# Normalising attention probabilities in place on GpSimd, instead of scaling the outputs by turned reciprocals

## The chip, the cores and the metric

The kernel runs on one core of one Trainium2 chip. The metric is the device time of one execution in microseconds: the median of several runs. All arrays are float32.

## What is computed

A normalised input goes through an attention layer and through a gated feed-forward branch (called FFN here); the output is the input plus the product of the two. The part that the change touches is the attention, with 4 sequences of 1024 tokens, 16 query heads of width 64 over 4 key heads, a causal window of 512 keys and 4 sink keys:

```python
att = jnp.einsum('bkgqd,bkjd->bkgqj', q, k) * scale
mask = _sliding_window_sink_mask(t)   # causal & j >= i - 511, or j < 4
att = jnp.where(mask[None, None, None, :, :], att, -jnp.inf)
att = jax.nn.softmax(att, axis=-1)
y = jnp.einsum('bkgqj,bkjd->bkgqd', att, v)
y = y.reshape(b, N_HEAD, t, HS).transpose(0, 2, 1, 3).reshape(b, t, c)
return y @ Wo.T
```

The softmax divides each row of exponentials by its sum. Since that division is by row (by query), it can be done on the exponentials before the second product, or on the product after it.

## The kernel before

The program has three stages: projections (up to about 949 us), attention with the recurrent FFN streamed beside it (949 to about 1745 us), and the output product with the gate. The change lies in the second stage, and in the few lines at the end of the first that prepare its first step.

**Steps.** A tile is 128 queries of one sequence. Tiles are taken in pairs (`PAIRED`): a far tile (5th to 8th of its sequence), which sees 512 window keys and 4 sink keys, 516 columns (`OWN`), and a near tile (1st to 4th), which sees 1 to 4 key tiles, 128 to 512 columns. The pair of sequence `b` and number `t` holds far tile 7 - t and near tile t, so the near tile has t + 1 key tiles. Each pair is worked off in four steps: two values of `m` (which pair of key heads) by two of `rp` (which pair of query heads in a group). So there are 16 pairs, 64 steps (`order`), numbered here from 0. Each step has, for each of its two tiles, four heads `(r, g)`: `r` is the query head of the pair, `g` the key head. "The first pair" is r = 0, both g.

**What a step does for a tile.** `scored` multiplies queries by keys into the PSUM tile `S` on TensorE (L299). For a far tile `merged` copies the own key tile's scores over the oldest one where the mask wants it (VectorE, L314). `maxed` adds the mask, scales, takes the row maximum and writes the result to the SBUF tile `pr` (VectorE, L335). `powered` takes the exponentials in place and their row sums into `sums` (ScalarE, L346, with a second instruction that reads the accumulator). `turned` transposes blocks of 128 keys of `pr` on TensorE into the PSUM tile `T`, two half transposes for each block and head (L365, `t<-ident,pr`), and copies them to SBUF as `pT` (ScalarE, L383). `values` multiplies `pT` by the values into a PSUM bank `yp` that the two tiles of the step share (L411). The far tile needs two things more: `led` makes a masked copy `lead` of its first key block (VectorE, L397), and `values_apart` adds the sink keys' share (L427) and `lead`'s share (L411).

**Normalising.** The exponentials are not divided. `inverted` takes the reciprocals of all 8 sums of the step in one instruction (VectorE, L475) and spreads each over 64 columns in SBUF (GpSimd, L477, 512 columns). `turned_extras` transposes five blocks of 128 columns in ten half transposes (L365): `held`, which holds the far tile's exponentials of the sink keys (copied out by `sinks_kept`, GpSimd, L354), and the four spread blocks. Its inner function `kept` copies the result to SBUF as the tile `extras`, named `e` in the profile (ScalarE, L497). `values_apart` reads the first block; `stored` multiplies `yp` by the other blocks on its way to SBUF (VectorE, L440). `sent` sends a finished tile's `y` to DRAM (GpSimd's queue, L447) after the second of two steps.

**Order.** The order on TensorE, VectorE, ScalarE and GpSimd is written out by hand (`tc.manual_schedule`), each engine works its list strictly in order, and the step's loop interleaves the values of step p with the scores and exponentials of step p + 1 (`far_next`, `near_next`). `streamed` puts blocks of the FFN between them (weights by DMA, products L1099); `small_products` and a few VectorE and GpSimd instructions (among them the small `trs` of L115) belong to it too.

There are two forms of a step. When the next near tile has one or two key tiles (`ride`), its scores ride in the free columns of the next far tile's `S`, and all four of its exponentials are taken before the step ends. The extras' transposes then go to the PSUM tile `T` (named `et` in the profile), and `kept` follows at once. This is called a riding step here. Otherwise, and in the last step, the form is a plain step: the near tile's scores have an `S` of their own at the step's end, the fourth of its exponentials is taken at the start of the following step, and the extras' transposes go into the free columns of the next far tile's `S`, where `kept` follows after `merged` and before `maxed`. `S`, `T` and `yp` are single tiles that each use must find released.

Of the kernel before, what the change touches and what calls it, by code (L numbers as in the profile page):

```python
# [8 lines left out]
F32 = mybir.dt.float32  # L9
AF = mybir.ActivationFunctionType  # L10
ALU = mybir.AluOpType
# [4 lines left out]
P = 128  # L16
N_HEAD = 16
N_KV = 4
HS = 64
WINDOW = 512  # L20
# [24 lines left out]
def recurrent_block_kernel(  # L45
# [206 lines left out]
    class Step:  # L252


        def __init__(self, i, m, rp, sums):
# [17 lines left out]
            self.sums = sums  # L273
            self.maxima = {}
            self.pT = {}

# [65 lines left out]
        def powered(self, *heads):  # L342

            for r, g in heads:
                low = self.pr[:, g, r, : self.cols]
                nc.scalar.activation(  # L346
                    low, low, AF.Exp, bias=self.maxima.pop((r, g)), scale=-1.0,
                    accum_out=self.sums[:, r, g : g + 1],
                )

        def sinks_kept(self):
# [71 lines left out]
        def values_apart(self):  # L423

            for r in range(PAIR):
                for _, rows, cols in self.quads():
                    nc.tensor.matmul(  # L427
                        self.y[rows, r * P : (r + 1) * P],
                        sink_values[self.b][:, r, cols], self.extras[:, 0, :],
                        start=False, stop=False, skip_group_check=True,  # L430
                    )
# [12 lines left out]

        def sent(self):
            if (self.rp + 1) * PAIR == GROUP:
# [13 lines left out]
    def steps_of(tiles, m, rp):  # L460
        sums = pools["first"].tile(
            [P, 2, PAIR, 2], F32, tag="sums", name=f"s{tiles[0]}_{m}_{rp}", bufs=3
        )
        return [Step(i, m, rp, sums[:, at]) for at, i in enumerate(tiles)], sums

    def summed_in_one_bank(far, near):

        y = pools["ps_y"].tile([P, 2, PAIR * P], F32, tag="y", name=f"yp{far.name}")
        far.y, near.y = y[:, 0, :], y[:, 1, :]

    def inverted(steps, sums):

        name = steps[0].name
        inverse = pools["px"].tile([P, 2 * PAIR * 2], F32, tag="inverse", name=f"i{name}", bufs=2)
        nc.vector.reciprocal(inverse, sums.rearrange("p s r g -> p (s r g)"))  # L475
        spread = pools["px"].tile([P, 2 * PAIR * 2, HS], F32, tag="spread", name=f"r{name}", bufs=1)
        nc.gpsimd.tensor_copy(  # L477
            spread, inverse.unsqueeze(2).to_broadcast([P, 2 * PAIR * 2, HS])
        )
        return spread.rearrange("p (s g) c -> p s (g c)", g=2)  # L480

    def turned_extras(steps, spread, behind):

        far, near = steps
        parts = [far.held, *(spread[:, s, :] for s in range(2 * PAIR))]
        if behind is None:
            ps = pools["ps_t"].tile([P, 2, WIDE], F32, tag="T", name=f"et{far.name}")
        else:
            ps = behind.S[:, 0, :, SCOLS:]
        for slot, src in enumerate(parts):  # L490
            far.in_halves(ps, slot, src, P)
        extras = pools["px"].tile([P, len(parts), P], F32, tag="extras", name=f"e{far.name}", bufs=1)
        far.extras = extras
        far.scales, near.scales = extras[:, 1 : 1 + PAIR, :], extras[:, 1 + PAIR :, :]

        def kept():
            nc.scalar.copy(  # L497
                extras.rearrange("p s (h q) -> p h s q", h=2),
                ps[:, :, : len(parts) * HS].rearrange("p h (s q) -> p h s q", q=HS),
            )  # L500

        return kept
# [17 lines left out]
    with ExitStack() as a:  # L520
# [445 lines left out]
        with tc.manual_schedule():  # L966
# [4 lines left out]
            for at, (kind, pair) in enumerate(passes):  # L971
# [35 lines left out]
                for k, i in enumerate(OUTER):  # L1007
# [16 lines left out]
                    if end and k == 3:  # L1024
# [10 lines left out]
                        def scores(step, rs):  # L1035
# [5 lines left out]
                        first_scores = iter((  # L1041
                            lambda: scores(far, (0,)), lambda: scores(far, (1,)),
                            far.sinks_kept, lambda: scores(near, both),
                        ))
            for part in first_scores:
                part()
# [11 lines left out]
    with ExitStack() as a:  # L1058

        px = pools["px"] = a.enter_context(tc.tile_pool(name="px", bufs=1))  # L1060
        pools["odd"] = a.enter_context(tc.tile_pool(name="odd", bufs=1))
        ps_t = pools["ps_t"] = a.enter_context(tc.tile_pool(name="ps_t", bufs=1, space=PSUM))
        ps_f = a.enter_context(tc.tile_pool(name="ps_f", bufs=1, space=PSUM))
        pools["ps_y"] = a.enter_context(tc.tile_pool(name="ps_y", bufs=1, space=PSUM))
# [669 lines left out]
```

## Time and profile before

| | |
|---|---|
| median of 3 runs | 2138.59 us (2137.0 to 2141.21) |
| profiled execution | 2139.05 us |
| its span | 2137.3 us |
| mean granted TensorE clock | 0.995 |
| TensorE matmul busy | 2076.3 us (97%) |
| VectorE busy | 1495.8 us (70%) |
| ScalarE busy | 916.5 us (43%) |
| GpSimd busy | 448.4 us (21%) |

The page gives busy time, the chain of work that ended last, groups of instructions by line, and, for an idle engine, what ended the idle time. `PE` is TensorE's matmuls, `PEld` its weight loads, which overlap them, `DVE` VectorE, `ACT` ScalarE, `POOL` GpSimd, `SP` SyncE. In a group's row, `out<-in` are the program's names, then come shapes and count, then busy time and the mean of one in ns, then the idle time before the group and what ended it. In a timeline, a row has its start, its length, the engine and line, and in brackets the idle time of the engine before it with its releaser. Matmuls are pipelined and their ends are modelled, so a busy TensorE may still wait a little. Between 950 and 1700 us TensorE is busy nearly all of the time and GpSimd for 5 to 11 us in each 50.

### The profile page before, as it was taken

The page shows a single profiled execution, that of the slowest core. Times are in us where ns is not written, and L with a number is a line of the kernel's source. Part 1 is how long each engine was busy: PE and PEld are TensorE (multiplying, and loading weights), DVE is VectorE, ACT ScalarE, POOL GpSimd, SP SyncE. Part 2 cuts the span into 40 slices and gives each one's busy share as a digit, 9 for nine tenths or more (in the row PEclk, how much of TensorE's full clock was granted, in tenths as well). Part 3 has the DMA queues.
Part 4 walks back from the last instruction along what each step waited for, and adds up shares of the span by engine and source line. Part 5 has one row for each costly group of instructions (what it writes and reads, how often), then busy time and mean ns, then how long its engine had stood idle before and what let it go on. Part 6 is the DMA issues. An engine that isn't in the chain of part 4 may idle for free.

```text
span 2137.3 us, 43582 instructions
## 1 busy us (share of the span) xinstructions
PE 2076.3 (97%) x17586; PEld 1418.0 (66%) x17586; DVE 1495.8 (70%) x3092; ACT 916.5 (43%) x1840; POOL 448.4 (21%) x641
## 2 busy tenths in 40 slices
PE   7999999999999999999999999999999989999999
PEld 6888888888888888875555655555565544444443
DVE  5867588888877888876556555666665547777766
ACT  4343212111110000037777777777777744333332
POOL 3232315435241021141111111111111101111111
PEclk9999999999999999999999999999999999999999
DMA  8696322433554234258778988768578536666653
GB/s 297 248 370 218 104 99 99 163 114 124 224 188 138 99 110 166 79 190 290 261 237 240 319 250 243 256 198 301 185 251 284 182 146 180 167 169 191 172 157 98
DMA packets 215201, 417.20 MB, mean 195 GB/s; under 512 B 13796, under 2 KB 97844, under 8 KB 209880
## 3 DMA queue, kind: packets, MB, share of 16 engines
q1 hardware_dynamic: 171432, 266.12, 38.8%
q0 software_dynamic: 28288, 91.41, 13.8%
q10 hardware_dynamic: 15280, 56.89, 7.1%
q8 instruction: 138, 2.26, 0.4%
q14 instruction: 63, 0.52, 0.1%
HBM read 309.22 MB, written 121.93 MB: 202 GB/s over the span
## 4 chain that ended last, share of the span: by engine, by line
PE 83%; DVE 6%; issue 4%; ACT 4%; POOL 2%; DMA 1%; SPq 0%; ACTq 0%; POOLq 0%; DVEq 0%
PE u L1572 17%; PE u_q L899 16%; PE u_g L899 13%; PE S L299 10%; PE yp L411 8%; PE d_ps L1099 6%; PE t L365 5%; PE u L679 4%; PE yp L427 1%; DVE pr L335 1%; ACT pr L346 1%; ACT pT L383 1%; DVE t_g L915 1%; DVE f L852 1%; PE xtp L595 1%
## 5 line engine op out<-in xcount | busy, mean ns | idle before, releaser
L346 ACT ACTIVATE pr<-pr,nm 128x516 f32<-128x516 f32 (+4 forms) x512 | 325.5, 638 | 86.8 <-DVE nm L335 85.7
L335 DVE CUSTOM_DVE_ANT_0 pr<-S,near_mask 128x516 f32<-128x516 f32 (+4 forms) x512 | 275.7, 590 | 98.2 <-PE S L299 56.0
L383 ACT COPY pT<-t 128x1024 f32<-128x1024 f32 (+1 forms) x224 | 212.0, 946 | 116.5 <-PE t L365 114.5
L299 PE MATMUL S<-kT,qT 64*128 64x512 f32 (+4 forms) x1536 | 246.4, 446 | 4.0 <-DVE i L475 2.4
L411 PE MATMUL yp<-pT,v 128*32 128x256 f32 x3328 | 215.2, 382 | 5.1 <-ACT pT L383 4.5
L899 PE MATMUL u_q<-f,wq_again 128*128 128x256 f32 x896 | 203.2, 379 | 0.0
L899 PE MATMUL u_g<-wg,f 128*128 128x256 f32 x864 | 195.7, 380 | 4.5 <-DVE t_g L915 4.5
L365 PEld LDWEIGHTS t<-ident,pr 64*128 64x128 f32 x3328 | 126.1, 140 | 90.6 <-issue 68.6
L411 PEld LDWEIGHTS yp<-pT,v 128*32 128x32 f32 x3328 | 104.1, 110 | 123.4 <-issue 51.7
L899 PEld LDWEIGHTS u_q<-f,wq_again 128*128 128x128 f32 x896 | 170.0, 190 | 23.3
L899 PEld LDWEIGHTS u_g<-wg,f 128*128 128x128 f32 x864 | 163.8, 190 | 28.2 <-DVE t_g L915 6.2
L299 PEld LDWEIGHTS S<-kT,qT 64*128 64x128 f32 x1536 | 127.6, 190 | 79.2 <-issue 69.8
L1572 PE MATMUL u<-wo_sb,y 128*128 128x512 f32 x384 | 170.1, 592 | 0.5 <-DVE y L440 0.5
L365 PE MATMUL t<-ident,pr 64*128 64x64 f32 x3328 | 153.1, 230 | 4.0 <-ACT pr L346 1.8
L314 DVE COPY_PREDICATED S<-own_keys,S 128x256 f32<-128x256 uint32 x128 | 54.9, 429 | 131.2 <-PE S L299 92.3
L945 ACT COPY t_q<-u_q 128x512 f32<-128x512 f32 x28 | 16.4, 586 | 275.4 <-PE u_q L899 275.4
L1572 PEld LDWEIGHTS u<-wo_sb,y 128*128 128x128 f32 x384 | 72.9, 190 | 92.4 <-issue 91.4
L915 DVE TENSOR_TENSOR t_q<-u_q,t_q 128x512 f32<-128x512 f32 x128 | 88.2, 689 | 63.8 <-PE u_q L899 49.3
L915 DVE TENSOR_TENSOR t_g<-u_g,t_g 128x512 f32<-128x512 f32 x128 | 87.9, 687 | 40.8 <-PE u_g L899 35.8
L1572 PE MATMUL u<-wo_t,s 128*128 128x512 f32 x256 | 112.5, 592 | 0.0
L346 ACT ACTIVATION_READ_ACCUMULATOR pr<-pr,nm 128x1 f32 x512 | 96.6, 189 | 0.0
L477 POOL COPY r<-i 128x512 f32<-128x512 f32 x64 | 47.7, 745 | 217.4 <-DVE i L475 208.0
(284 smaller groups left out, 3560.6 us busy)
## 6 DMA issues: line engine op xcount, KB each, us to landing
d_w<-in_d_w_dram SPq DMA_DIRECT2D x128, 1024.0 KB, 8.0
xT<-xT_dram SPq DMA_DIRECT2D x24, 1024.0 KB, 5.6
xn<-in_x_dram ACTq DMA_DIRECT2D x34, 512.0 KB, 5.4
xT_dram<-xT POOLq DMA_DIRECT2D x32, 512.0 KB, 6.0
qT<-q_dram SPq DMA_DIRECT2D x64, 256.0 KB, 5.8
y_dram<-y POOLq DMA_DIRECT2D x64, 256.0 KB, 5.8
y<-y_dram SPq DMA_DIRECT2D x32, 512.0 KB, 5.3
g<-g_dram SPq DMA_DIRECT2D x32, 512.0 KB, 11.2
```

The costliest lines, as they stand in the source:

```text
L299: nc.tensor.matmul(S[:, g, :], qTs[self.i, self.m][half, self.rp * PAIR + r, :], kT[half, self.m, keys, start:], start=True, stop=True,)
L314: nc.vector.copy_predicated(S[:, dst, :, 0:P], masks["own"].bitcast(mybir.dt.uint32).unsqueeze(1).to_broadcast([P, 2, P]), S[:, dst, :, OW ...
L335: nc.vector.tensor_tensor_reduce(out=low, in0=S[:, src, g, :cols], in1=self.mask, scale=-1.0 / HS**0.5, scalar=-NEG, op0=ALU.add, op1=ALU.min,
L346: nc.scalar.activation(low, low, AF.Exp, bias=self.maxima.pop((r, g)), scale=-1.0, accum_out=self.sums[:, r, g : g + 1],)
L365: nc.tensor.transpose(ps[:n, h, slot * HS : (slot + 1) * HS], src[rows], ident[rows, rows])
L383: nc.scalar.copy(pT.rearrange("p k g c -> p (k g c)")[:, : slots * P].rearrange("p (s h q) -> p h s q", h=2, q=HS), ps[:, :, : slots * HS] ...
L411: nc.tensor.matmul(self.y[rows, :], v[:, cols], pT[:, g, :], start=first, stop=last, skip_group_check=True,)
L679: nc.tensor.matmul(bank, left[n][i].rearrange("p a (k q) -> p a k q", k=2)[:, c // 2, c % 2, j * P : (j + 1) * P], kv7[i][:, c, :], start= ...
L899: nc.tensor.matmul(bank[:, t * QD : (t + 1) * QD], stationary[:, at : at + P], moving[:, c * QD : (c + 1) * QD], start=(first and c == 0 a ...
L915: nc.vector.tensor_add(dst, in0, in1)
L1099: nc.tensor.matmul(ps[j * QUAD : (j + 1) * QUAD, :], lhs[:, k, :], moving(w), start=(u == 0), stop=(u == len(blocks) - 1),)
L1572: nc.tensor.matmul(bank, left[n][i][:, c, j * P : (j + 1) * P], wo7[i][:, c, :], start=(first and c == 0), stop=(c == KH - 1), skip_group_ ...
```

## The change

The reciprocals are taken in pieces, as soon as the sums of one or two heads are there. A new method `normed` multiplies a head's exponentials in `pr` in place by their reciprocals, on GpSimd: all four heads of the near tile, and the two of the far tile's first pair. The far tile's second pair is still scaled on the way out. So only two reciprocals of a step are spread (128 columns instead of 512), and `turned_extras` transposes two blocks in four half transposes instead of five in ten. The tile `extras` is now made once, filled with ones; its middle block stays at one and is what the first pair is multiplied by. The near tile's `stored` becomes a copy.

In riding steps the extras' transposes go into the next far tile's `S` where they fit, that is when the next near tile has one key tile, and to `T` otherwise; `kept` follows `merged` in both cases. The spread of the next far tile's reciprocals is issued at the end of the step before.

```diff
+        def normed(self, *heads):
+            for r, g in heads:
+                low = self.pr[:, g, r, : self.cols]
+                nc.gpsimd.tensor_scalar(
+                    low, low, self.inverse[:, r, g : g + 1], None, ALU.mult
+                )
...
-            nc.vector.tensor_tensor(
-                state[self.i][:, at : at + PAIR, :],
-                self.y.rearrange("p (r q) -> p r q", r=PAIR), self.scales, ALU.mult,
-            )
+            dst = state[self.i][:, at : at + PAIR, :]
+            y = self.y.rearrange("p (r q) -> p r q", r=PAIR)
+            if self.far:
+                nc.vector.tensor_tensor(dst, y, pools["extras"][:, 1:, :], ALU.mult)
+            else:
+                nc.vector.tensor_copy(dst, y)
...
-    def inverted(steps, sums):
...
+    def inverted(of, first, last):
+        nc.vector.reciprocal(*(t[:, first:last] for t in of))
+
+    def spread(far):
+        far.scale = pools["px"].tile([P, 2, HS], F32, tag="spread", name=f"r{far.name}", bufs=1)
         nc.gpsimd.tensor_copy(
-            spread, inverse.unsqueeze(2).to_broadcast([P, 2 * PAIR * 2, HS])
+            far.scale, far.inverse[:, 1, :].unsqueeze(2).to_broadcast([P, 2, HS])
         )
...
-    def turned_extras(steps, spread, behind):
-        far, near = steps
-        parts = [far.held, *(spread[:, s, :] for s in range(2 * PAIR))]
+    def turned_extras(far, behind, at):
+        parts = [far.held, far.scale.rearrange("p g c -> p (g c)")]
...
-            ps = behind.S[:, 0, :, SCOLS:]
+            ps = behind.S[:, 0, :, at:]
...
+                        def far_kept():
+                            inverted(sums_now, 0, 2)
+                            far.normed((0, 0), (0, 1))
+                            far.sinks_kept()
+                        def near_kept():
+                            inverted(sums_now, 2, 6)
+                            near.normed((0, 0), (0, 1))
...
+        pools["extras"] = px.tile([P, 1 + PAIR, P], F32, name="extras")
+        nc.gpsimd.memset(pools["extras"], 1.0)
+        spread(far)
```

and in the step's loop:

```diff
                 if rode:
-                    spread = inverted((far, near), sums_now)
+                    inverted(sums_now, 6, 8)
+                    near.normed((1, 0), (1, 1))
+                else:
+                    inverted(sums_now, 6, 7)
+                    near.normed((1, 0))
                 if more:
                     far_next.merged((0,))
                     far_next.maxed((0,))
...
                 if not rode:
-                    spread = inverted((far, near), sums_now)
+                    inverted(sums_now, 7, 8)
+                    near.normed((1, 1))
                 far.led()
+                if more:
+                    inverted(sums_next, 0, 1)
+                    far_next.normed((0, 0))
                 streamed(1, 1)
...
                     near_next.riding(1, far_next)
-                    turned_extras((far, near), spread, None)()
+                    fits = near_next.cols + PAIR * HS <= 2 * WINDOW - SCOLS
+                    kept = turned_extras(
+                        far, far_next if fits else None, SCOLS + near_next.cols
+                    )
+                    inverted(sums_next, 1, 2)
+                    far_next.normed((0, 1))
                     far_next.merged((1,))
+                    kept()
                     far_next.maxed((1,))
                     near_next.maxed((1,))
+                    inverted(sums_next, 4, 6)
+                    near_next.normed((0, 0), (0, 1))
                     far_next.powered((1, 0), (1, 1))
...
-                    kept = turned_extras((far, near), spread, far_next if more else None)
+                    kept = turned_extras(far, far_next if more else None, SCOLS)
                     if more:
                         far_next.merged((1,))
                     kept()
                     if more:
                         far_next.maxed((1,))
+                        inverted(sums_next, 1, 2)
+                        far_next.normed((0, 1))
                         far_next.powered((1, 0), (1, 1))
...
                 near.stored()
+                if more:
+                    if ride:
+                        inverted(sums_next, 2, 4)
+                        spread(far_next)
+                    else:
+                        inverted(sums_next, 2, 6)
+                        spread(far_next)
+                        near_next.normed((0, 0), (0, 1))
```

More of the change, by code (lines that the diff above doesn't have):

```diff
@@ L252, in recurrent_block_kernel, with __init__ @@
     class Step:
-        def __init__(self, i, m, rp, sums):
+        def __init__(self, i, m, rp, sums, inverse):
             self.name = f"{i}_{m}_{rp}"
@@ L272, in __init__ @@
             )
-            self.sums = sums
+            self.sums, self.inverse = sums, inverse
             self.maxima = {}
@@ L428, in values_apart @@
                         self.y[rows, r * P : (r + 1) * P],
-                        sink_values[self.b][:, r, cols], self.extras[:, 0, :],
+                        sink_values[self.b][:, r, cols], pools["extras"][:, 0, :],
                         start=False, stop=False, skip_group_check=True,
@@ L463, in steps_of @@
         )
-        return [Step(i, m, rp, sums[:, at]) for at, i in enumerate(tiles)], sums
+        inverse = pools["first"].tile(
+            [P, 2, PAIR, 2], F32, tag="inverse", name=f"i{tiles[0]}_{m}_{rp}", bufs=3
+        )
+        steps = [Step(i, m, rp, sums[:, at], inverse[:, at]) for at, i in enumerate(tiles)]
+        return steps, [t.rearrange("p s r g -> p (s r g)") for t in (inverse, sums)]
     def summed_in_one_bank(far, near):
@@ L469, in summed_in_one_bank @@
         far.y, near.y = y[:, 0, :], y[:, 1, :]
-    def inverted(steps, sums):
[L473 to L476, printed above, removed]
+    def inverted(of, first, last):
+        nc.vector.reciprocal(*(t[:, first:last] for t in of))
+    def spread(far):
+        far.scale = pools["px"].tile([P, 2, HS], F32, tag="spread", name=f"r{far.name}", bufs=1)
         nc.gpsimd.tensor_copy(
-            spread, inverse.unsqueeze(2).to_broadcast([P, 2 * PAIR * 2, HS])
+            far.scale, far.inverse[:, 1, :].unsqueeze(2).to_broadcast([P, 2, HS])
         )
-        return spread.rearrange("p (s g) c -> p s (g c)", g=2)
-    def turned_extras(steps, spread, behind):
-        far, near = steps
-        parts = [far.held, *(spread[:, s, :] for s in range(2 * PAIR))]
+    def turned_extras(far, behind, at):
+        parts = [far.held, far.scale.rearrange("p g c -> p (g c)")]
         if behind is None:
@@ L488, in turned_extras @@
         else:
-            ps = behind.S[:, 0, :, SCOLS:]
+            ps = behind.S[:, 0, :, at:]
         for slot, src in enumerate(parts):
             far.in_halves(ps, slot, src, P)
-        extras = pools["px"].tile([P, len(parts), P], F32, tag="extras", name=f"e{far.name}", bufs=1)
-        far.extras = extras
-        far.scales, near.scales = extras[:, 1 : 1 + PAIR, :], extras[:, 1 + PAIR :, :]
         def kept():
             nc.scalar.copy(
-                extras.rearrange("p s (h q) -> p h s q", h=2),
+                pools["extras"][:, ::2, :].rearrange("p s (h q) -> p h s q", h=2),
                 ps[:, :, : len(parts) * HS].rearrange("p h (s q) -> p h s q", q=HS),
@@ L1039, in scores @@
                             step.powered(*((r, g) for r in rs for g in range(2)))
+                        def far_kept():
[5 more added lines that the diff above has]
+                            near.normed((0, 0), (0, 1))
                         first_scores = iter((
                             lambda: scores(far, (0,)), lambda: scores(far, (1,)),
-                            far.sinks_kept, lambda: scores(near, both),
+                            far_kept, lambda: scores(near, both), near_kept,
                         ))
@@ L1400, in recurrent_block_kernel @@
                     near_next.riding(1, far_next)
-                    turned_extras((far, near), spread, None)()
+                    fits = near_next.cols + PAIR * HS <= 2 * WINDOW - SCOLS
+                    kept = turned_extras(
+                        far, far_next if fits else None, SCOLS + near_next.cols
+                    )
+                    inverted(sums_next, 1, 2)
+                    far_next.normed((0, 1))
                     far_next.merged((1,))
+                    kept()
                     far_next.maxed((1,))
                     near_next.maxed((1,))
+                    inverted(sums_next, 4, 6)
+                    near_next.normed((0, 0), (0, 1))
                     far_next.powered((1, 0), (1, 1))
```

## The prediction

> **What bounds the kernel.** I read the page's busy shares and chain first, then the chain of waits, the timeline step by step, groups by shape and waits.
>
> ```profile
> PE 2076.3 (97%) x17586; PEld 1418.0 (66%) x17586; DVE 1495.8 (70%) x3092; ACT 916.5 (43%) x1840; POOL 448.4 (21%) x641
> ...
> PE 83%; DVE 6%; issue 4%; ACT 4%; POOL 2%; DMA 1%; SPq 0%; ACTq 0%; POOLq 0%; DVEq 0%
> ```
>
> TensorE carries the program and GpSimd is the idle engine. The chain of waits inside one attention step (1436.62 to 1450.50 us):
>
> ```profile
> 1440.34 0.65 PE t L365 x16
> 1440.99 1.14 PE S L299 x8
> 1442.13 0.31 PE S L365 x10
> 1442.43 0.99 PE d_ps L1099 x8
> 1443.43 0.86 PE yp L411 x16
> ```
>
> The ten transposes of the extras (`S L365 x10`) lie on the path with nothing beside them. The change makes them four. The next two fences are the timeline, first a plain step (next near tile of 3 or 4 key tiles, or the last step: 33 of 64), then a riding one (1 or 2 key tiles: 31):
>
> ```profile
> 1664.81 0.43 DVE L314 COPY_PREDICATED S<-own_keys,S 128x256 f32<-128x256 uint32 x1 [1.38 <-PE S L365]
> 1665.28 0.69 ACT L497 COPY e<-S 128x640 f32<-128x640 f32 x1
> 1666.00 0.70 DVE L335 CUSTOM_DVE_ANT_0 pr<-S,near_mask 128x516 f32<-128x516 f32 x1 [0.76 <-ACT e L497]
> ```
>
> ```profile
> 1162.70 0.43 DVE L314 COPY_PREDICATED S<-own_keys,S 128x256 f32<-128x256 uint32 x1 [1.03 <-PE S L299]
> 1163.00 0.69 ACT L497 COPY e<-et 128x640 f32<-128x640 f32 x1 [0.31 <-PE et L365]
> 1163.17 0.70 DVE L335 CUSTOM_DVE_ANT_0 pr<-S,near_mask 128x516 f32<-128x516 f32 x1
> ...
> 1164.63 0.71 ACT L346 ACTIVATE pr<-pr,nm 128x516 f32<-128x516 f32 x1
> 1164.75 0.26 PEld L365 LDWEIGHTS t<-ident,pr 64*128 64x128 f32 x6 [0.41 <-issue]
> ...
> 1165.48 0.53 PE L365 MATMUL t<-ident,pr 64*128 64x64 f32 x10 [0.33 <-ACT pr L346]
> ```
>
> Where the extras lie in the score tile S, merging (L314) waits for their transposes and the maxima (L335) wait for ScalarE's copy; where they lie in `et`, neither does. And in the riding step TensorE starts the next far tile, does six transposes and waits for the last far exponential: there the path is scores, merge, maxima, exponentials, not the transposes.
>
> **What goes.** Sixteen transposes take 0.65 us, 0.041 each; six fewer save 0.25 us (by the ten at 0.31, 0.19). ScalarE's copy shrinks from 640 to 256 columns. Its other copies take 1007 ns for 1024 and 586 for 512 (0.82 ns a column), so it falls from 690 to about 375 ns.
>
> Plain steps: the exponentials are done in time (the last far one 2.4 us or more before the step's end), so 33 x 0.25 = 8.25 us. In steps 45, 59, 61, 62 TensorE also waits 0.24 to 0.51 us for that copy (L427 <- ACT e), and in 9, 24, 39 2.7 us behind table loads: 0.32 off the former where there is that much, 0.07 more than the 0.25 off the latter: 1.3. The last step waits for the copy twice: 0.5.
>
> Riding steps with a next near tile of two: extras stay in `et`. In 12 of 16 the last far exponential ends 0.18 us or more before the next start (or the extras themselves are late, step 53): 12 x 0.25 = 3.0. In steps 3, 38, 51, 52 it ends 0.24 to 0.68 after it: nothing.
>
> Riding steps with a next near tile of one (15): here the extras now go into S (772 + 128 columns fit). Merge waits for four more transposes, 0.15, and the maxima for the copy, 0.40 (0.76 idle above for 690 ns, less 0.32): 0.55 us in the chain. Step 17 above is one. The last far exponential ends, against the next start, at +0.53, +0.68, +0.68, +0.68, +0.25, +0.25, +0.24, +0.25 in eight: +0.55 each, 4.4 us lost. In four it ends at -0.61: covered, 4 x 0.25 = 1.0 won. In the three from a near tile of four to one of one (15, 31, 47) the near tile's second `pT` copy stands behind those exponentials (TensorE already waits up to 1.38 us for it): 3 x 0.55 = 1.65 lost.
>
> **What comes.** No `tensor_scalar` on GpSimd is in the trace. Its rows:
>
> ```profile
> L866 POOL TENSOR_TENSOR t_g<-t_g,gate_b_sb 128x512 f32<-128x512 f32 x32 | 52.4, 1638 | 186.2 <-DVE t_g L915 185.8
> L477 POOL COPY r<-i 128x512 f32<-128x512 f32 x64 | 47.7, 745 | 217.4 <-DVE i L475 208.0 <-PE t L365 9.2 <-PE S L299 0.2
> ...
> L354 POOL COPY held<-pr 128x16 f32<-128x16 f32 x64 | 12.6, 197 | 369.5 <-ACT pr L346 369.5
> ```
>
> The pass has one tensor input, so I take the copies: 0.61 us at their shortest for 512 columns and 0.197 for 16 make 0.84 ns a column: 0.62 us for 516, 0.51 for 384, 0.40 for 256, 0.29 for 128. The upper end is 1.64 us for 512. Two far and four near passes and a smaller spread add about 2.6 us of GpSimd to a step of 9 to 16, some 165 us in all, covered by its idle time if each pass makes its deadline. Plain steps: the far passes end some 3 us before the next step. The near tile's last exponential comes at +2.4 to +2.9 us, its reciprocal ends at 4 to 4.7, the pass at 5.5; the near transposes start at 8.3 or later (7.3 in the last step). Riding steps: the reciprocal ends at 1.0 to 3.8, two short passes and a y transfer queued ahead of them (0.55) end by 5.5 in the worst, transposes start at 4.7 to 6.0, late with late. Exceptions are 31 and 47: the last near reciprocal ends at 4.56 and 5.59, the pass 0.2 + 0.87 later, and the transpose that needs it is due at 5.15 and 5.77: 0.5 + 0.9 = 1.4 us lost.
>
> Four more reciprocals on VectorE (L475, 0.20 us, the next instruction starts 0.12 later) wait for exponentials. Behind them stand the merge and maxima, but these then wait for scores anyway (0.7 to 1.5 us idle before L314), so I take zero; without cover up to 0.5 us a step. Behind the passes on GpSimd stand `held`, y's transfers and FFN's four `trs`: zero, at most 0.7 us four times.
>
> ```profile
> 1662.80 0.64 DVE L397 TENSOR_TENSOR lead<-pT,lead_keys 128x512 f32<-128x512 f32 x1
> ...
> 1663.04 0.87 POOL L477 COPY r<-i 128x512 f32<-128x512 f32 x1 [2.50 <-DVE i L475]
> ...
> 1169.26 0.62 POOL L477 COPY r<-i 128x512 f32<-128x512 f32 x1
> ```
>
> Beside `lead` the copy took 0.87 us, alone 0.62; hence the 0.87 above. Passes can hold up `lead` in turn; it has over 2 us until L411 needs it.
>
> The Trainium skill, SBUF — State Buffer, "Who interferes with whom", says more than these rows: a VectorE instruction with two SBUF inputs and a GpSimd one that reads SBUF shut each other out whole, whichever comes second, so `lead` could lose a whole pass; by the rows a pass loses 0.25. The sum is the same by both, since `lead` has the 2 us. Its GPSIMD Engine Reference, "Engine selection", speaks against elementwise work on GpSimd (about half VectorE's pace), yet calls one-input work roughly line-rate; by that, at 1.2 GHz, a pass of 512 would take an estimated 0.43 us and the sum gain 0.4. No row here shows it.
>
> **Sum**: -8.25 - 1.3 - 0.5 - 3.0 - 1.0 + 4.4 + 1.65 + 1.4 = -6.6 us. The profiled execution took 2139.05 (span 2137.3 and 1.75 around it), 0.46 above the median of 2138.59: 2132.4 on it, 2132.0 as a median. With 0.19 for 0.25 in the 49 steps the gain shrinks to 3.7; the forecast's own range is 2126 to 2136.
>
> **Rivals.**
> *Slow passes, slower.* At 1.64 us for 512 columns the last near pass of a four-tile step ends 1.1 (first near reciprocal) + 0.3 (spread) + 0.55 (transfer) + 0.3 (hand-overs) + 4 x 1.64 = 8.8 us after the step's start. In 13 plain steps it is due at 8.5: 4 us lost; in 15, 31, 47 at about 5.4: 10 in place of 1.4. Net +6: 2144.6. It decides from about 1.55 us a pass; each 0.1 more costs 16 x 0.4 = 6.4. For it: the 1638 ns row. Against: that row reads two tensors. 0.17.
> *Chain in all riding steps, no change.* The copy now stands after the merge everywhere; if the maxima wait for it with `et` too, or reciprocals are uncovered, the two-tile steps lose their 3.0 and up to 0.3 each, 3.6: 2138.6. Against: the row at 1163.17 started while the copy from `et` ran. 0.23.
> *No new wait, faster.* If the one-tile steps keep their chain, 8 + 3 lose nothing and TensorE gains there too: 6.05 + 2.8 more: 2123. Against: all 32 L335 <- ACT e waits. 0.12.
>
> **Numbers.** Forecast 0.48. A measurement of this kernel tells about 0.2% (4.3 us): faster means under 2134.3. The forecast gives 0.41 of that, the fast rival 0.12, the neutral one 0.02: 0.55. Slower is most of the slow rival, 0.14, and 0.04 of the neutral one: 0.18; the rest, 0.27, is no change. The range reaches from the fast rival to the slow one: 2122 to 2145.
>
> **Right or wrong.** Right: `S` or `et` transposes fall from 640 to 256, the copy to near 375 ns, GpSimd's passes to about 0.6 us, plain steps 0.25 us shorter, L335 waits for ACT in 47 steps instead of 32, at 0.4 us each, and one-tile steps 0.5 longer. Wrong: transposes (`t L365`) that wait for GpSimd in many steps, passes over 1 us, or riding steps that shorten.

## The result and the profile after

The changed kernel took 2161.53 us (median; 2158.35 to 2163.42), beside 2138.82 us of the kernel before in the same runs: a ratio of 1.0104, 95% interval 1.0087 to 1.0122. It is slower by 1.0%. The forecast was 2132.0 us, and the range, 2122 to 2145, does not hold the time. The profiled execution took 2162.85 us (span 2161.1), 23.8 more than the one before.

The page of the changed kernel, its busy shares and the two groups that matter most:

```profile
PE 2079.8 (96%) x17202; PEld 1414.3 (65%) x17202; DVE 1516.4 (70%) x3346; ACT 897.5 (42%) x1840; POOL 900.0 (42%) x1026
...
L355 POOL TENSOR_SCALAR pr<-pr,i 128x516 f32<-128x516 f32 (+4 forms) x384 | 479.4, 1260 | 124.8 <-DVE i L487 88.5
...
L373 PE MATMUL t<-ident,pr 64*128 64x64 f32 x3328 | 159.9, 231 | 23.6 <-POOL pr L355 16.0
```

GpSimd's busy time has doubled (448.4 to 900.0 us): 452 us more, not the 165 on which the prediction counted. The passes alone are 479 us, and the transposes of `pr` now wait for them: TensorE stood still for 16.0 us. The same passes by shape, in the groups of GpSimd:

```profile
L355 POOL TENSOR_SCALAR pr<-pr,i 128x512 f32<-128x512 f32 x64 | 100.7, 1585 | 0.3
L355 POOL TENSOR_SCALAR pr<-pr,i 128x384 f32<-128x384 f32 x64 | 82.5, 1300 | 0.3
...
L355 POOL TENSOR_SCALAR pr<-pr,i 128x128 f32<-128x128 f32 x64 | 38.1, 606 | 30.0 <-DVE i L487 25.1 <-DVE th L1193 1.7 <-DVE th L1200 1.6
```

A pass over 512 columns takes 1.585 us. It is hardly faster than the 1.638 us of the product with two full inputs that the prediction had as its upper end, and 2.5 times the copy that it took.

**Where the time went.** In the trace a step can be timed from the first transpose of its far tile to that of the next step. All 64 steps together grew from 793.9 to 818.2 us, by 24.3; outside attention nothing changed to speak of. Steps are numbered from 0.

| steps | after minus before, us |
|---|---|
| 12, 28, 44 | +5.60, +4.77, +4.52 = +14.9 |
| 15, 31, 47 (four key tiles to one) | +2.16, +3.87, +2.35 = +8.4 |
| 1, 4, 18 | +2.27, +2.48, +1.26 = +6.0 |
| 17, 35, 49, 50, 51 | +0.50 to +0.52 each = +2.5 |
| 46, 53 | +0.68, +1.60 = +2.3 |
| 24 | -1.56 |
| the other 47 | -8.2, most of them -0.17 to -0.21 each |

So most of 47 steps did what was forecast of them, on a smaller scale, and 16 paid for it. What happens in step 12 (1094.03 to 1113.77 us) is seen in GpSimd's timeline of the changed kernel:

```profile
1095.98 3.11 POOL L355 TENSOR_SCALAR pr<-pr,i 128x512 f32<-128x512 f32 x2
1099.04 0.36 POOL L178 COPY kT<-kT 128x32 f32<-128x32 f32 x1
1099.34 0.52 POOL L184 MEMSET sinks<- 128x512 f32 x1
1100.16 2.36 POOL L188 DMA_DIRECT2D sinks<-v_dram  x4 [0.29 <-POOL sinks L184]
1102.51 0.59 POOL L457 DMA_DIRECT2D y_dram<-y  x1
1103.13 6.21 POOL L355 TENSOR_SCALAR pr<-pr,i 128x512 f32<-128x512 f32 x4
```

Lines 178 to 188 are `load_sinks`, a function of the kernel before that the prediction did not mention. Once for each of the next three sequences, at the top of a step with a near tile of four key tiles, it copies sink keys, clears a buffer and starts four transfers through GpSimd's own queue: 3.5 us from 1099.04 to 1102.5. The near tile's second pair of passes stands behind that and behind `y`'s transfer, and so starts at 1103.13. Their transposes on TensorE, in its timeline:

```profile
1102.95 0.28 PE L373 MATMUL t<-ident,pr 64*128 64x64 f32 x2
1104.76 0.34 PE L373 MATMUL t<-ident,pr 64*128 64x64 f32 x4 [1.54 <-POOL pr L355]
1106.30 0.79 PE L373 MATMUL t<-ident,pr 64*128 64x64 f32 x10 [1.20 <-POOL pr L355]
1106.89 3.73 PE L299 MATMUL S<-kT,qT 64*128 64x512 f32 x8
...
1123.21 1.94 PE L299 MATMUL S<-kT,qT 64*128 64x512 f32 x8
```

The two waits are one pass each, 2.7 us together. Then the near tile's eight score matmuls take 3.73 us. In the next step the same eight take 1.94 (the last row), as in the kernel before: TensorE's clock has fallen. The view by windows gives each window's length, the busy times of PE, PEld, DVE, ACT and POOL, then the granted clock, the DMA share and GB/s:

```profile
1080.00:1094.00 14.00, 14.00 (x212) 7.62 (x208) 9.25 (x33) 10.59 (x24) 9.11 (x9) 1.00 0.83 263
1094.00:1108.00 14.00, 10.84 (x148) 6.22 (x146) 7.50 (x26) 8.40 (x20) 12.00 (x14) 0.92 0.62 192
1108.00:1116.00 8.00, 8.00 (x116) 4.32 (x116) 3.04 (x10) 4.64 (x10) 2.98 (x4) 0.72 0.13 39
```

The granted clock is 1.00, then 0.92, then 0.72. Over the whole run it is 0.991, before it was 0.995: 0.009 of 2161.1 against 0.005 of 2137.3 is 19.4 against 10.7 us of clock, 8.7 us more (8.4 by the unrounded means). That is about the most that the clock can have added to this execution, a third of the 24.3. In steps 12, 28 and 44, taken whole, the granted clock is 0.83, 0.91 and 0.91 over 19.74, 18.91 and 18.14 us, and 1.00 in all three before: at most 3.4 + 1.7 + 1.6 = 6.7 of their 14.9 us. The rest, 8.2 or more, is waiting.

The same `load_sinks` could be read in GpSimd's timeline of the kernel *before*. There it delayed nothing: behind it and `y`'s transfer GpSimd idles 2.59 us until a reciprocal comes.

```profile
1088.97 0.22 POOL L178 COPY kT<-kT 128x32 f32<-128x32 f32 x1
1089.11 0.54 POOL L184 MEMSET sinks<- 128x512 f32 x1
1089.94 2.29 POOL L188 DMA_DIRECT2D sinks<-v_dram  x4 [0.30 <-POOL sinks L184]
1092.49 0.58 POOL L447 DMA_DIRECT2D y_dram<-y  x1 [0.26 <-DVE y L440]
1095.66 0.89 POOL L477 COPY r<-i 128x512 f32<-128x512 f32 x1 [2.59 <-DVE i L475]
```

Step 60 has the same form as 12, 28 and 44 but no next sequence to load: it became 0.64 us shorter. Step 1 is the same story with the FFN's four bias-row transfers and two memsets (L1097 to L1104, 3.3 us) ahead of the passes, steps 4 and 18 the reverse: there the FFN's `trs` stands *behind* passes and comes late.

### The profile page after: what moved, and what is told of

Read it like the earlier page. It is cut to its first block, busy times and chain, and to the rows that moved or that the text cites. A ratio compares the mean times of both kernels' runs of the same rounds, so it can differ in the third digit from the quotient of the medians.

```text
span 2161.1 us, 43630 instructions
## 1 busy us (share of the span) xinstructions
PE 2079.8 (96%) x17202; PEld 1414.3 (65%) x17202; DVE 1516.4 (70%) x3346; ACT 897.5 (42%) x1840; POOL 900.0 (42%) x1026
## 5 line engine op out<-in xcount | busy, mean ns | idle before, releaser
L355 POOL TENSOR_SCALAR pr<-pr,i 128x516 f32<-128x516 f32 (+4 forms) x384 | 479.4, 1260 | 124.8 <-DVE i L487 88.5
L335 DVE CUSTOM_DVE_ANT_0 pr<-S,near_mask 128x516 f32<-128x516 f32 (+4 forms) x512 | 275.7, 590 | 113.8 <-PE S L299 65.2
L299 PE MATMUL S<-kT,qT 64*128 64x512 f32 (+4 forms) x1536 | 252.4, 455 | 3.9 <-DVE i L487 2.5
L373 PE MATMUL t<-ident,pr 64*128 64x64 f32 x3328 | 159.9, 231 | 23.6 <-POOL pr L355 16.0
L876 POOL TENSOR_TENSOR t_g<-t_g,gate_b_sb 128x512 f32<-128x512 f32 x32 | 52.4, 1637 | 186.2 <-DVE t_g L925 186.1
L1593 POOL DMA_DIRECT2D out_dram<-g x30 | 25.9, 864 | 224.8 <-DVE g L1581 203.6
```

The lines of the kernel that those rows point to most:

```text
L299: nc.tensor.matmul(S[:, g, :], qTs[self.i, self.m][half, self.rp * PAIR + r, :], kT[half, self.m, keys, start:], start=True, stop=True,)
L335: nc.vector.tensor_tensor_reduce(out=low, in0=S[:, src, g, :cols], in1=self.mask, scale=-1.0 / HS**0.5, scalar=-NEG, op0=ALU.add, op1=ALU.min,
L355: nc.gpsimd.tensor_scalar(low, low, self.inverse[:, r, g : g + 1], None, ALU.mult)
L373: nc.tensor.transpose(ps[:n, h, slot * HS : (slot + 1) * HS], src[rows], ident[rows, rows])
L876: nc.gpsimd.tensor_add(v, v, gate_b_sb[:, at : at + QD].unsqueeze(1).to_broadcast([P, 2, QD]))
```

## The experiments

The main theory is the queue: passes are 2.5 times as long as assumed, and where other work stands ahead of them in GpSimd's list, the near transposes wait. Its rivals are the chain (the extras' transposes put into `S` in riding steps hold up merge and maxima) and the port (passes stretch VectorE's instructions). Ratios are to the kernel before in the same runs; diffs are against the changed kernel, but for one.

**Copies in place of products.** If only the length of the pass is wrong in the prediction, a pass as long as a copy must bring the forecast back.

```diff
-                nc.gpsimd.tensor_scalar(
-                    low, low, self.inverse[:, r, g : g + 1], None, ALU.mult
-                )
+                nc.gpsimd.tensor_copy(low, low)
```

> Each pass becomes a plain in-place copy on GpSimd at the same place and over the same columns, so the near heads and the far tile's first pair are not divided by their sums. Theory Q (queue: a pass costs 1.57 us for 512 columns, and TensorE waits where GpSimd has other work ahead of a near pass or little time before it): passes near 0.62 us, no wait of TensorE for GpSimd over 0.5 us, about 28 us less than the changed kernel: 2133 us. Theory C (chain: the longer path merge, copy, maxima, exponentials and the extra reciprocals cost the time): at most 3 us less, 2158 or more. Theory P (port: GpSimd's passes hold up VectorE): VectorE is held up in proportion to the passes' time, about half of the loss stays: 2147.

Measured: 2133.76 us, ratio 0.9985 [0.9975, 0.9994], which is 3.2 us less than before [1.3 to 5.3]. The copies' groups, and TensorE's weight loads in the view of waits (who waits, for whom, us in all, times, longest), last the changed kernel's own row of it:

```profile
L355 POOL COPY pr<-pr 128x516 f32<-128x516 f32 x128 | 94.4, 744 | 142.0 <-ACT pr L346 140.2
L355 POOL COPY pr<-pr 128x512 f32<-128x512 f32 x64 | 38.2, 630 | 0.0
...
PEld t L371 <- POOL pr L355: 4.9, 12, 0.4
```

```profile
PEld t L373 <- POOL pr L355: 28.0, 40, 2.2
PE t L373 <- POOL pr L355: 16.0, 15, 2.1
```

With passes of the assumed length TensorE's own waits for GpSimd are gone, steps 12, 28 and 44 are 5.7, 4.8 and 4.7 us shorter than in the changed kernel, and the time is near the 3.7 us of gain that the prediction gave for transposes at 0.19. `load_sinks` stands where it stood. The port theory asked for 2147 here, and in the changed kernel itself the maxima (L335, 516 columns) take 693 ns as before: it is not what costs the time. The copies need no reciprocal either, so this run alone does not part the pass' length from its wait for the reciprocal; the run with broadcast products below does.

**Near passes on VectorE.**

```diff
-                nc.gpsimd.tensor_scalar(
+                engine = nc.gpsimd if self.far else nc.vector
+                engine.tensor_scalar(
```

> The near tile's passes move from GpSimd to VectorE, the far tile's stay. Theory Q: waits of TensorE for GpSimd go, VectorE gains 1.3 to 2 us of work a step; 2132 to 2140 us. Theory C: VectorE's list gets longer and with it the chain: 2165 us or more. Theory P: the near passes on VectorE are themselves stretched beside far passes (single rows well over 0.6 us) and the time stays above 2145.

Measured: 2158.57 us, 1.0100 [1.0085, 1.0115]. Steps 12, 28 and 44 lost 5.0, 4.2 and 3.6 us of their surplus and 15, 31, 47 lost 1.7, 3.4 and 1.0, as the queue theory wants. But 29 other steps became 0.2 to 1.3 us longer, 14.6 us together, and the ratio is nearly the same. The passes on VectorE, by shape, and a wait of TensorE's next scores that the changed kernel does not have in its upper rows:

```profile
L356 DVE TENSOR_SCALAR pr<-pr,i 128x512 f32<-128x512 f32 x64 | 30.3, 494 | 1.7
...
PE S L299 <- DVE i L488: 11.3, 18, 2.0
```

A pass takes 0.494 us there, a third of GpSimd's, yet it stands in VectorE's list ahead of what the next scores wait for. The queue theory's figure for this run is missed, since it took room on VectorE for granted: busy 70% of the span, that engine had none at that place.

**`load_sinks` behind the near passes.** The call moves from the top of the step to just ahead of `far.led()`.

```diff
-                    if t == 3 and b + 1 < B:
-                        load_sinks(b + 1)
...
+                if within == 0 and t == 3 and b + 1 < B:
+                    load_sinks(b + 1)
```

> Only the place of load_sinks in the order changes: behind the near passes of the same step instead of ahead of them (three steps: 12, 28, 44). Theory Q: these steps go from 18.1 to 19.7 us back to 13.5 to 14, about 15 us in all: 2146.5. Theories C and P: no change, 2161.

Measured: 2149.39 us, 1.0057 [1.0042, 1.0072]. Steps 12, 28 and 44 are back to 0.07 to 0.2 us below the kernel before: their whole +14.9, the clock's part included, goes with the place of `load_sinks`, at this length of the pass. About 3.5 us came back in the steps after them: 13, 29 and 45 grew by 1.1 to 1.3 against the changed kernel, with waits of 0.9 to 1.1 us for passes, because the passes of the next far tile now stand behind the same transfers. Neither place has slack for 3.5 us of other work on GpSimd.

**Extras never in the far tile's `S` in riding steps.**

```diff
-                    fits = near_next.cols + PAIR * HS <= 2 * WINDOW - SCOLS
+                    fits = False
```

> In riding steps the extras always go to the transposes' tile, as in the kernel before; the maxima then need not wait for the copy. Theory Q: only one-key riding steps with a late last exponential gain, 6 to 9 times 0.55 us: 2157. Theory C: most of the loss goes, 2146 or less. Theory P: no change.

Measured: 2153.88 us, 1.0080 [1.0065, 1.0095]. Steps 17, 35, 49, 50 and 51 lose their +0.5 (17 loses 0.85), 15, 31 and 47 0.5 each, 4.4 us together. The five stand behind one-key riding steps (16, 34, 48, 49, 50): the next step waits for the late exponential after its first six transposes, so the time falls there. The mechanism of the chain theory is there, at the price that the prediction gave it (0.55), but it is a small part of the loss: 1.0104 less 1.0080 is 5 of 22 us. The wait that it stands on, in the view of waits of the changed kernel and then of this one:

```profile
DVE pr L335 <- ACT extras L507: 29.6, 47, 3.1
```

```profile
DVE pr L335 <- ACT extras L507: 23.0, 32, 3.1
```

The 15 waits that the prediction had announced (47 in place of 32) are the 15 that go.

**Two late passes on VectorE.** Only the near tile's second pair in the steps from four key tiles to one.

```diff
-                    near.normed((1, 0))
+                    near.normed((1, 0), engine=nc.vector if ride else None)
...
-                    near.normed((1, 1))
+                    near.normed((1, 1), engine=nc.vector if ride else None)
```

> The changed kernel with only the last two near passes of steps 15, 31 and 47 on VectorE (6 of 384 passes). Theory Q: these steps lose 1.2 to 1.8 us of waiting each and what follows from it, 4 to 6 us in all: 2156. Theories C and P: no change.

Measured: 2154.79 us, 1.0087 [1.0070, 1.0105]. Six of 384 passes moved: 15, 31 and 47 are 1.7, 3.0 and 1.0 us shorter, 5.7 together; step 32 gives 1.2 of it back. What remains in step 47 (0.7 us) is a wait for the pass on VectorE.

**Three forms of the pass beside each other.** For the durations alone: far tile as it is; the near tile's first pair by a constant of 1.0; its second pair by the reciprocals as a broadcast tensor.

```diff
+                if self.far:
+                    nc.gpsimd.tensor_scalar(
+                        low, low, self.inverse[:, r, g : g + 1], None, ALU.mult
+                    )
+                elif r == 0:
+                    nc.gpsimd.tensor_scalar(low, low, 1.0, None, ALU.mult)
+                else:
+                    nc.gpsimd.tensor_tensor(
+                        low, low, self.inverse[:, r, g : g + 1].to_broadcast([P, self.cols]),
+                        ALU.mult,
+                    )
```

> What the form of a pass costs: the far passes as they are (multiplication by a scalar read per partition), the near tile's first pair multiplied by the constant one (so not divided by its sums), its second pair as a two-input product with the reciprocal broadcast along the row. If the scalar operand is the cost, the constant form runs at the copies' 0.63 us for 512 columns and the broadcast form at 1.6; if the arithmetic is, both take 1.5 or more.

It ran at 2147.98 us, once. The groups by shape:

```profile
L356 POOL TENSOR_SCALAR pr<-pr,i 128x516 f32<-128x516 f32 x128 | 200.8, 1572 | 108.9 <-DVE i L495 66.2 <-ACT pr L346 30.6 <-DVE mean L1219 7.0
L360 POOL TENSOR_SCALAR pr<-pr 128x512 f32<-128x512 f32 x32 | 47.7, 1502 | 0.0
L362 POOL TENSOR_TENSOR pr<-pr,i 128x512 f32<-128x512 f32 x32 | 36.0, 1148 | 0.5 <-DVE i L495 0.3
```

The operand in memory is not what makes the pass slow: with a constant it takes 1.50 us. The kind of instruction is: as a product with a second input that is one number per partition the same work takes 1.15 us, less than with the scalar form and less than with two full inputs (1.64). Neither of the two expected outcomes had that.

**All passes as broadcast products.**

```diff
-                nc.gpsimd.tensor_scalar(
-                    low, low, self.inverse[:, r, g : g + 1], None, ALU.mult
+                nc.gpsimd.tensor_tensor(
+                    low, low, self.inverse[:, r, g : g + 1].to_broadcast([P, self.cols]),
+                    ALU.mult,
```

> The changed kernel with only the form of the pass changed: two-input products with the reciprocal broadcast, 1.15 us instead of 1.57 for 512 columns. Theory Q: the loss shrinks with the pass, not in proportion: each near pass of a four-tile step is due at the same time, so steps 12, 28, 44 lose 4 x 0.42 us less and 15, 31, 47 likewise: 10 to 15 us less, 2148. Theory C: no change, 2160. Theory P: 0.42 of 1.57, about 6 us less, 2155.

Measured: 2140.41 us, 1.0012 [1.0003, 1.0021]. A group and the wait:

```profile
L355 POOL TENSOR_TENSOR pr<-pr,i 128x512 f32<-128x512 f32 x64 | 68.7, 1096 | 3.3 <-DVE i L488 3.0
...
PE t L374 <- POOL pr L355: 5.1, 8, 1.2
```

Same computation, same order, same dependencies; 0.49 us less for 512 columns is worth 0.92% of the time, 19.7 us (1.0104 less 1.0012, from different runs of the kernel before), more than the 10 to 15 that were expected. With the copies (0.63 us) and the change itself (1.585) this gives three points: against before -3.2, +2.6 and +22.2 us at 0.63, 1.10 and 1.585 us. The cost is no straight line: the first 0.47 us cost 5.8, the next 0.49 cost 19.7. Slack is used up, and behind the waits the clock falls: the granted clocks of the two profiled executions, 0.991 and 0.996, allow some 11 of the 19.7 us to be the clock's.

**No passes at all, extras in `T` in riding steps.** The ceiling of what fewer transposes can bring.

```diff
-            for r, g in heads:
...
+            pass
...
-                    fits = near_next.cols + PAIR * HS <= 2 * WINDOW - SCOLS
+                    fits = False
```

> The changed kernel without any pass (near heads and the far tile's first pair are not divided) and with the extras always in the transposes' tile: what is left of the change is six transposes fewer, a shorter copy and the reciprocals. Theory Q: 0.19 us a step, 12 us in all, and 1 us of waits for the copy: 2125. If six transposes are worth the 0.25 of the prediction: 2121. Theory C: the reciprocals eat most of it, 2133 or more.

Measured: 2127.00 us, 0.9944 [0.9929, 0.9959]. Attention takes 780.1 us, 13.8 less than before, with nearly all plain and two-key steps at -0.18 or -0.19. So 0.19 is the price of six transposes, the lower of the two figures in the prediction, 12 us in 64 steps, and 0.6% is about all that the idea can give when the passes cost nothing.

**The sink transfers on another queue, in the kernel before.** A control for the two combinations below: `load_sinks` is split, its four transfers and the FFN's bias rows go to SyncE's queue, and its buffers are cleared once, ahead of attention.

```diff
-        sinks = pools["first"].tile([P, PAIR, KVD], F32, tag="sinks", name=f"sinks{b}", bufs=2)
-        nc.gpsimd.memset(sinks, 0.0)
+    def load_sinks(b):
+        sinks = sink_tiles[b % 2]
...
-                nc.gpsimd.dma_start(
+                nc.sync.dma_start(
```

> Control: the kernel before, with the same transfers on SyncE's queue and the buffers zeroed once. Theories Q, C and P: TensorE did not wait for GpSimd there, no change, within 2 us of the kernel before.

Measured: 2138.67 us, 1.0007 [0.9994, 1.0021]. By itself the edit does nothing.

**Repairs together.** The changed kernel with that edit, the copy of the sink keys moved behind the near passes, `fits = False`, and the two late passes on VectorE.

> The changed kernel with GpSimd's queue cleared where TensorE waited for it: the sink rows' and bias rows' transfers go to SyncE's queue, their buffers are zeroed once, the copy of the sink keys stands behind the near passes, the last two near passes of steps 15, 31 and 47 run on VectorE, and the extras always go to the transposes' tile in riding steps. Theory Q: 15 us (steps 12, 28, 44) + 6 (15, 31, 47) + 6 (extras) + 2 (step 1) less than the changed kernel: 2132, faster than the kernel before. Theory C: 2150 or more. Theory P: the passes still hold up VectorE, 2145.

Measured: 2134.30 us, 0.9992 [0.9981, 1.0003]: the 1.0% are gone, and the kernel cannot be told from the one before; the gain that was expected beyond that is not shown. In its trace step 4 still has +2.5 and step 18 +1.15, where `trs` waits behind passes.

**Repairs, broadcast products, and two passes later.** As above, all passes on GpSimd as broadcast products, and in riding steps the next near tile's first pair behind the FFN's `trs`.

```diff
                     inverted(sums_next, 4, 6)
-                    near_next.normed((0, 0), (0, 1))
...
+                    near_next.normed((0, 0), (0, 1))
                     far.stored()
```

> As the kernel best, with two changes more: the passes on GpSimd are two-input products with the reciprocal broadcast along the row (1.15 us for 512 columns instead of 1.57), and in riding steps the first near passes stand behind the FFN's small GpSimd instruction, not ahead of it. Theory Q: the waits left in steps 1, 4, 18 and 46 (0.5 to 2.5 us each) go: 3 to 4 us less than best, 2131, 0.3% faster than the kernel before. Theory C: like best, no difference from the kernel before.

Measured: 2135.03 us, 0.9978 [0.9969, 0.9986]: faster than the kernel before, by 0.2%, and 1.3% below the change as it was made. TensorE's weight loads now wait for passes 2.8 us in all:

```profile
PEld t L380 <- POOL pr L362: 2.8, 7, 0.4
```

## Why the prediction was wrong

**What held.** The six fewer transposes came off the path in most of 47 steps. The copy of the extras is 371 ns (375 forecast); the row below is the group of the changed kernel. Maxima wait for it in 47 steps. One-key riding steps without cover cost 0.5 us (0.55 forecast). Steps 45, 61 and 62 gained 0.5 (0.25 + 0.32); the fourth of that kind, 59, did not (+0.09). `lead` went from 663 to 725 ns on average, and TensorE has no wait for it. It never lost a whole pass: 40 of the 64 ran beside one, and the longest took 1.02 us, against 0.69 without.

```profile
L507 ACT COPY extras<-S 128x256 f32<-128x256 f32 x47 | 17.4, 371 | 14.1 <-DVE S L314 8.2 <-DVE S L321 5.2
```

**The step that failed** is the sentence "The pass has one tensor input, so I take the copies: ... 0.62 us for 516". The two nearest rows lay at 0.61 and 1.64 us; the choice went by the number of inputs, and the instruction took 1.57. The copies show that this was enough: with passes of that length the time is 3.2 us below before, within the forecast's own range, and the broadcast products show that at equal dependencies the length alone decides. Here the row of arithmetic on GpSimd was the one to go by, not the row of a copy. The Trainium skill's GPSIMD Engine Reference, "Engine selection", on which the prediction had noted that one-input work is roughly line-rate, fits the copies (0.87 ns a column, 0.63 us for 512) and not this instruction (2.55 ns a column); the measurement decides.

**The rival that had the sign had a quarter of the size.** "Slow passes, slower" gave 2144.6 us for 1.64 us, 6.0 above before where 22.7 were measured, and put its loss in plain steps where passes are due at 8.5 us and in 15, 31, 47. The latter lost 8.4 us in all (10 forecast for the passes there, and 1.65 for the chain). Of the former, 13, 14, 29, 30, 45, 60, 61 and 62 gained, and where only passes and one `y` transfer stood in the list nothing was lost; 12, 28, 44 and 46 lost, where other work shares the list. Three causes were missing, all of them visible before:

- `load_sinks` ahead of the passes, +14.9 us with what the clock adds there. The sentence "Behind the passes on GpSimd stand `held`, y's transfers and FFN's four `trs`" lists what waits behind the passes; what stands *ahead* of them was counted as one `y` transfer of 0.55. Moving `load_sinks` cleared those steps.
- The FFN's work on GpSimd, in steps 1, 4 and 18, +6.0 us: transfers and memsets ahead in step 1, `trs` behind in 4 and 18 (and in 46, with 0.42 us of waiting for a pass), where "at most 0.7 us four times" counted a pass of 0.62.
- TensorE's clock, at most 8.7 us, inside the figures above and in step 53 (clock 1.00 before, 0.89 after), for which the prediction had no term. The kernel before shows it in step 24.

**The size of the gain** was too large as well: 0.25 us a step from the mean of sixteen transposes, 0.19 measured, which is the row of the ten that the change thins out. In 49 steps that is 2.9 us, as the prediction's own lower figure had it. The last step gained nothing (0.5 forecast): it ends in waits for ScalarE and VectorE that the fewer transposes do not move. The one surprise to the good is step 24, 1.56 us shorter: its granted clock was 0.82 before and is 0.90.

**What stays open.** The clock's share is bounded by the granted clock and not measured: no run changes the clock alone. And the last combination stays 7.3 us above the run without passes (0.9978 against 0.9944); by the granted clocks of the two profiled executions, 0.994 and 0.997, as much as some 6 us of that can be the clock, and what the passes themselves cost was not tried.

## What to carry to other kernels

An operation that the trace does not show is priced by the row of the same kind of work on the same engine (here arithmetic, not a copy), and a forecast whose sign turns between two such rows is no forecast until one of them is excluded. Work that is moved onto an idle engine joins a list that is worked in order: read everything in that list between the operand and the deadline, rare instructions and DMA issues too, since a step that comes three times can cost more than the other sixty gain. Before giving up, try the same arithmetic in another form: it was worth 0.9% here.

## What the runs showed of the hardware

**GpSimd's price goes by the kind of instruction.** From 128 to 512 columns of float32 the scalar product goes from 0.606 to 1.585 us, 2.55 ns a column, (1585 - 606) / 384; the product with a broadcast second input from 0.409 to 1.096, 1.79 ns; a copy from 0.295 to 0.630, 0.87 ns. A scalar that is a constant saves 5% (1.502). VectorE does the same scalar product in 0.494 us for 512 columns.

**A transfer through GpSimd's queue holds its list for about 0.59 us** (four of `sinks` in 2.36, one `y` in 0.59; the others of the kernel before take 0.53 to 0.86 on average), and passes behind it wait that long.

**TensorE's clock falls when TensorE stands idle for about half of a window of 3.41 us, and no one wait need be that long.** In step 12 of the changed kernel waits of 1.54 and 1.20 us with 0.34 us of work between them were followed by 6.83 us at half clock. In the traces' record of the clock it is 1.00 or 0.50, and within a trace the stretches at 0.50 start at whole multiples of 3.413 us from each other. So time can be read in windows of 3.41 us that are counted from such a start. In step 12 TensorE is busy for 1.30 us of one window, and the next is at half clock:

```profile
1102.26:1105.67 3.41, 1.30 (x26) 0.62 (x18) 1.51 (x5) 1.47 (x4) 3.38 (x4) 1.00 1.05 322
1105.67:1109.09 3.42, 2.79 (x16) 1.70 (x18) 0.00 (x0) 1.01 (x1) 3.42 (x3) 0.50 0.53 202
```

In the thirteen traces, between 950 and 1760 us, 60 windows at full clock had half clock behind them, and TensorE was busy for 0.20 to 0.55 of each; the 2947 others were busy for 0.43 or more of theirs. The Trainium skill, TensorE: Matmul & The Clock Gate, Part 1, says that the clock halves after at least one idle window of about 3.4 us. The length agrees. But the window need not be idle, so 3.4 us is not a safe limit for a wait in this kernel. Nor is any one wait a sure trigger: step 9 waits 2.56 to 2.59 us for ScalarE's copy in several of these kernels. In the changed kernel (first) the edge of a window divides this wait; in the one with broadcast products (second) it lies in one window:

```profile
1057.88:1061.30 3.42, 2.42 (x28) 1.28 (x28) 1.20 (x4) 3.39 (x5) 3.42 (x3) 1.00 0.82 307
1061.30:1064.71 3.41, 1.85 (x42) 1.39 (x44) 1.71 (x6) 2.63 (x7) 0.09 (x2) 1.00 0.04 14
```

```profile
1058.41:1061.82 3.41, 0.84 (x28) 0.49 (x24) 0.51 (x1) 2.84 (x6) 0.09 (x1) 1.00 0.18 68
1061.82:1065.23 3.41, 3.41 (x38) 1.99 (x28) 1.30 (x6) 2.54 (x5) 1.75 (x3) 0.50 0.03 7
```

The clock stays at 1.00 in the one and falls to 0.50 in the other, and step 9 is 1.2 us longer in the latter. A price for a wait on TensorE has therefore to include, as a chance, the stretch at half clock behind it.
